# A graph layer's edge loop: the first set's sorting drawn in smaller portions over more parts, and dst compared with node numbers by tensor_tensor from PSUM

## Chip, cores and metric

The kernel runs on one core of one Trainium2 chip. The metric is the device time of one execution in microseconds, as the median of several executions; less is better. Beside it stands one profiled execution, from which every duration below is taken. The engines are named as the profile has them: PE (TensorE matmul), PEld (its weight load), DVE (VectorE), ACT (ScalarE), POOL (GpSimd) and SP (SyncE, here a queue that issues DMAs).

## The reference

x has 12500 nodes of 128 features. There are 412500 edges (200000 random pairs in both directions and a loop at each node), sorted by dst.

```python
theta = x[dst] - x[src]
w = sigmoid(relu(theta @ W1 + b1) @ W2 + b2)
w_theta = w * theta
agg = segment_sum(w_theta, dst, num_segments=n_nodes)
indeg = segment_sum(ones((dst.shape[0], 1)), dst, num_segments=n_nodes)
out = layernorm(x + agg + indeg * (x @ W4 + b4))
```

Since (x[dst] - x[src]) @ W1 is x[dst] @ W1 - x[src] @ W1, the product is needed once for each node and not once for each edge.

## The kernel before

**Table.** The nodes are taken in 14 chunks of up to 1024. `table_chunk` loads rows of x, turns them on PE (L607), multiplies by W1 (L612), and stores x @ W1 beside x in the DRAM table z, one row of 256 floats for a node (DVE copies the product, L615, ACT copies x, L616, SP stores, L617).

**Parts and blocks.** The edges are cut into 372 parts of up to 1024, handled as 8 tiles of 128 edges; two parts make a block, whose dst lie within 96 consecutive nodes. `gather(s)` issues eight indirect DMAs on POOL's queue (L328), each fetching 128 rows by the indices of the part's src: out of x for parts 0 to 7 (`NH = 8`), out of z from part 8 on. A gather of part s also waits until the compute of part s - 6 (`LAG`) has come to the corresponding place (`steps_of`); the main loop calls `gather(s + 4)` (`AHEAD`) in part s. For parts 0 to 7 each gather waits for a step of the table instead, so that they spread over it. The gathered rows lie in nine buffers.

In the loop over parts, a part's compute is: `one_hot` builds oh, a matrix that has a one where an edge belongs to one of three groups of 41 nodes' places; `spread_y` multiplies it with the block's own product y (L714), which gives each edge its dst's product in PSUM; `weights` subtracts the gathered product (DVE L757), applies relu and w2 (L758), sums (L761), and scales the gathered rows by the sigmoid (ACT L762, L764); `one_hot_w` compares 96 node places with each edge's dst (L724) and `add_up` sums the scaled rows by node on PE (L827). Parts 0 to 7 compute the product themselves from the gathered x (`both`, L735 to L742) in place of L757. Each block also has picks for y (`part_y`, L670 to L680), a compare of edges to often used rows that stay in SBUF (`hot_one_hot`, L779 and L784), and its own totals (`total`, of which L843 writes the columns `own`) and normalization.

**Sorting.** Parts 0 to 17 (`PLAIN`) take their edges as they are stored. The other 354 parts belong to three sets of 128, 128 and 98 parts, each of which is prepared at once by the generator `place`: each partition holds one part's 1116 edges; edges to the 1152 first nodes are taken out (64 of the largest keys by `max` and `match_replace`, L483 and L485), the others are moved together. Its steps are drawn with `next(steps)`, and each runs to the next `yield`. There are 79 draws for a set: 1 for columns, 3 for differences (which use the PSUM tile pw), 3 for keys, 16 for max and replace in turn, 1 for the hot edges (which stores hot_d), 6 for counts (pw again), 42 for shifting (seven rounds of six; L543, L545 and L547, whose scratch `bits` lies in PSUM), 1 that stores off_d, 1 that unpacks src, 4 for transposes into src_i and rel, and the last, which hands the set over. Part 18 is the first that uses the first set: its gathers, issued in the loop's part 14, need src_i, and the fetch of its block, in the same part, reads off_d and hot_d back.

The first set's draws stand behind table chunks 2 to 13 and at the head of the loop's first parts; the second and third set are drawn once a part, from parts 25 and 153 on.

**Order.** Instructions are emitted in the order of this program. SP's queue keeps that order exactly; on the other engines a planner may move an instruction ahead where its inputs allow. `after` puts what it holds behind given instructions of the same engine.

**The tile fix.** One PSUM tile of 512 columns holds constants and scratch: `iota_f` (96 columns, read by L724), `own` (128, written by ACT L843 and DVE L848), `nid` (9, read by L779) and the rest as `bits`, of which the shift uses up to 272 columns.

In parts from 18 on, `one_hot` compares `to_all` (the dst places of the part's edges, bf16 in SBUF, the same on all partitions) with `place_c` (one number per partition, SBUF) by one `tensor_scalar` of 123 x 1024 (L705).

The draws in the program:

```python
        while len(done) < len(chunks):
            chunk()
            gather_first()
            with after(done[-1]):
                for _ in range(6):
                    next(steps, None)
...
            if s % 2 == 0 or s < PLAIN - 3:
                for _ in range(3 if s < NH else 1):
                    next(steps, None)
```

Of the kernel before, what the change touches and what calls it, by code (L numbers as in the profile page):

```python
# [11 lines left out]
I32 = mybir.dt.int32  # L12
U16 = mybir.dt.uint16
AF = mybir.ActivationFunctionType
OP = mybir.AluOpType
# [3 lines left out]
P = 128  # L19
D = 128  # L20
# [3 lines left out]
WB = 96  # L24
SW = 41
# [8 lines left out]
NH = 8  # L34
FIRST = P // K
MORE = 2
PLAIN = FIRST + MORE
HS = 64
HT = 9
# [9 lines left out]
def gnn_resnorm(  # L49
# [37 lines left out]
    nc = tc.nc  # L87
# [10 lines left out]
    chunks = [(n0, P, TC) for n0 in range(0, N - P * TC + 1, P * TC)]  # L98
# [22 lines left out]
    def set_of(s):  # L121

        s0 = 0 if s < PLAIN else PLAIN + (s - PLAIN) // P * P
        return placed[s0], s - s0
# [76 lines left out]
    fix = cps.tile([P, 512], F32, name="fix")  # L201
    iota_f = fix[:, :WB].rearrange("p (o m) -> p o m", o=1)
    own = fix[:, WB:WB + D]
    nid = fix[:, WB + D:WB + D + HT]
    bits = fix[:, WB + D + HT:].bitcast(I32)
    w2_f = w2_r.rearrange("p (o m) -> p o m", o=1)

    YB = WB + 3
# [3 lines left out]
    def constants():  # L212

        nc.vector.tensor_copy(ident_b, ident)
        nc.vector.tensor_scalar_mul(wneg, wts[:, 0, :], -1.0)
        nc.scalar.activation(fix[:, :WB], iota_row[:, :WB], AF.Copy)

        def at_least(name, n, v=1.0):
            c = const.tile([P, 1], F32, name=name)
            nc.vector.tensor_scalar(c, iota_p, float(n), v, op0=OP.is_ge, op1=OP.mult)  # L220
            return c

        ge = [at_least(f"ge{i}", i * SW) for i in range(4)]
        m12 = const.tile([P, 1], F32, name="m12")
        nc.vector.tensor_sub(m12, ge[3], ge[1])
        m2 = const.tile([P, 1], F32, name="m2")
        nc.vector.tensor_sub(m2, ge[3], ge[2])


        for t in oh_buf:  # L230
            nc.vector.memset(t, 1.0)
        nc.vector.memset(to, 1.0)
        place_c = const.tile([P, 1], F32, name="place_c")
        nc.vector.tensor_add(place_c, ge[1], ge[2])
        nc.vector.tensor_scalar(place_c, place_c, -float(SW), None, op0=OP.mult)
        nc.vector.tensor_add(place_c, place_c, iota_p)

        yu_buf = [const.tile([P, 2, D], F32, name=f"yu{i}") for i in range(5)]
        bh = const.tile([P, D], BF16, name="bh")
        b1_s = const.tile([P, D], F32, name="b1_s")  # L240
        e_c = const.tile([P, 1], F32, name="e_c")
        nc.vector.memset(b1_s, 0.0)
        for i in range(3):
            nc.vector.tensor_copy(bh, b1_r)
            nc.vector.tensor_scalar(e_c, iota_p, float(WB + i), None, op0=OP.is_equal)
            nc.vector.scalar_tensor_tensor(b1_s, bh, e_c, b1_s, op0=OP.mult, op1=OP.add)
            nc.vector.tensor_sub(b1_r, b1_r, bh)
        for t in yu_buf:
            nc.vector.tensor_copy(t[WB:, 0, :], b1_s[WB:, :])

        ones_b = const.tile([3, P], BF16, name="ones_b")
        nc.vector.memset(ones_b, 1.0)
        b4_3 = const.tile([3, D], BF16, name="b4_3")
        b4_s = const.tile([3, D], F32, name="b4_s")
        nc.vector.memset(b4_s, 0.0)
        for i in range(3):
            nc.vector.tensor_copy(bh[:3], b4_r[:3])
            nc.vector.tensor_scalar(e_c[:3], iota_p[:3], float(i), None, op0=OP.is_equal)
            nc.vector.scalar_tensor_tensor(b4_s, bh[:3], e_c[:3], b4_s, op0=OP.mult, op1=OP.add)
            nc.vector.tensor_sub(b4_r[:3], b4_r[:3], bh[:3])  # L260
        nc.vector.tensor_copy(b4_3, b4_s)


        behind = const.tile([P, P], F32, name="behind")
        nc.vector.memset(behind, -4.0)
        for i in range(3):
            nc.vector.tensor_copy(behind[:WB, i * SW:(i + 1) * SW], lag[:WB, :SW])
        at = behind[WB:, 3 * SW:3 * SW + 3]
        nc.vector.tensor_scalar(at, lag[WB:, 3 * SW:3 * SW + 3], float(WB - 3 * SW), 4.25,
                                op0=OP.is_equal, op1=OP.mult)  # L270
        nc.vector.tensor_scalar(at, at, -4.0, None, op0=OP.add)

        place_w = const.tile([P, 1], F32, name="place_w")
        nc.vector.tensor_scalar(place_w, iota_p, -float(P), None, op0=OP.add)
        node_c = const.tile([P, 1], F32, name="node_c")
        nc.vector.tensor_scalar(node_c, iota_p, float(HT), None, op0=OP.mult)
        nc.vector.tensor_scalar(nid, iota_row[:, :HT], node_c, None, op0=OP.add)

        pair = const.tile([P, P // SUB], BF16, name="pair")
        nc.vector.tensor_add(pair, ident[:, 0::2], ident[:, 1::2])  # L280
        turn = []
        for h in range(SUB):
            turn.append(const.tile([P, 1], F32, name=f"turn{h}"))
            nc.vector.tensor_reduce(turn[h], ident[:, h::2], AX.X, OP.add)
        most = const.tile([P, 1], F32, name="most")
        nc.vector.memset(most, float(SW + HS))
        apart = const.tile([P, PM], F32, name="apart")
        nc.vector.tensor_scalar(apart, iota_row[:, :PM], 2048.0, None, op0=OP.mult)
        return (place_c, m12, m2, yu_buf, behind, ones_b, b4_3,
                (place_w, pair, turn, apart, most))  # L290
# [15 lines left out]
    def tiles(s):  # L306
        return K if s < NF else KT
# [269 lines left out]
    with tc.manual_schedule(engines={SP}), tc.tile_pool(name="work", bufs=2) as wp, tc.tile_pool(  # L577
# [43 lines left out]
        @contextmanager  # L621
        def after(instructions):

            with ExitStack() as stack:
                for i in instructions:
                    stack.enter_context(tc.issue_after(i.ins))
                yield
# [56 lines left out]
        def one_hot(s, half):  # L684


            n0, n1 = half * G, min(half * G + G, tiles(s))
            if half == 0:
                parts[s] = {"oh": oh_buf[s % 2]}
            oh = parts[s]["oh"]  # L690
            if s < PLAIN:
                (_, _, off), i = set_of(s)
                pd = ps_l.tile([P, G, P], F32, name="pd")
                pd = pd.rearrange("p k e -> p (k e)").bitcast(BF16)
                pd = pd.rearrange("p (k e) -> p k e", e=P)[:, :G, :]
                for k in range(n0, n1):
                    nc.tensor.transpose(pd[:, k - n0, :], off[:, k, i:i + 1].to_broadcast([P, P]),
                                        ident_b)
                nc.vector.tensor_scalar(oh[:3 * SW, n0:n1, :], pd[:3 * SW, :n1 - n0, :],
                                        place_c[:3 * SW], None, op0=OP.is_equal)  # L700
            elif half == 0:
                n = tiles(s)
                b, h = divmod(s, SUB)
                at = blocks[b]["to_all"].rearrange("p h (k e) -> p h k e", e=P)
                nc.vector.tensor_scalar(oh[:3 * SW, :n, :], at[:3 * SW, h, :n, :],  # L705
                                        place_c[:3 * SW], None, op0=OP.is_equal)

        def spread_y(s):

# [172 lines left out]
        xts, done = [], []  # L882

        def chunk():
            c = len(done)
            xts.extend(table_load(i) for i in range(len(xts), min(c + 3, len(chunks))))
            done.append(table_chunk(c, xts[c]))
# [4 lines left out]
        def gather_first():  # L892

            while gathered[0] < AHEAD and (gathered[0] + 1) * len(chunks) <= (len(done) + 1) * NH:
                gather(gathered[0])
                gathered[0] += 1
# [8 lines left out]
        with after(done[1]):  # L905
            place_first_dst(0, FIRST, ps_l, dst_f)
            place_c, m12, m2, yu_buf, behind, ones_b, b4_3, hot_c = constants()
            place_w = hot_c[0]
# [5 lines left out]
        while len(done) < len(chunks):  # L914
            chunk()
            gather_first()
            with after(done[-1]):
                for _ in range(6):
                    next(steps, None)
        with after(done[7]):  # L920
            bases(FIRST, NS, ps_l)
# [5 lines left out]
        with after(done[9]):  # L927
            window(0)
            for s in (0, 1):
                one_hot(s, 0)  # L930
                one_hot(s, 1)
                if s == 0:
                    spread_y(0)
        for s in range(NS + 2):
# [7 lines left out]
                    hot_t, z[:HOT, :].rearrange("(p t) d -> p t d", t=HT))  # L942
                nc.scalar.activation(hot_t[:, :, :D], hot_t[:, :, :D], AF.Copy, scale=-1.0)
            if s % 2 == 0 or s < PLAIN - 3:
                for _ in range(3 if s < NH else 1):
                    next(steps, None)
            b = s // SUB
            if s % SUB == 0:
# [5 lines left out]
            if s >= NH and s + 2 < NS:  # L954
                one_hot(s + 2, 0)
# [228 lines left out]
```

## Time and profile before

| | us |
|---|---|
| median of three runs | 3919.13 (3914.03 to 3920.94) |
| the profiled execution, device time | 3919.01 |
| its span, first to last instruction | 3917.2 (mean granted clock 0.806) |

| engine | busy us | share of the span | instructions |
|---|---|---|---|
| PE | 2667.6 | 68% | 15349 |
| PEld | 2252.2 | 57% | 15349 |
| DVE | 2829.5 | 72% | 5501 |
| ACT | 1594.4 | 41% | 5226 |
| POOL | 2866.5 | 73% | 2978 |

The page's chain of waits, followed back from the last instruction, has 34% DVE, 22% DMA, 19% PE, 16% ACT, 6% issue and 2% POOL. It is to be read with care: at each step it goes to what released a wait last, and where several engines work in step it changes between them.

By stretches (from the busy times of windows, us of each engine):

| window | length | PE | DVE | ACT | POOL |
|---|---|---|---|---|---|
| 60 to 80 | 20 | 0.77 | 18.38 | 2.54 | 3.73 |
| 100 to 120 | 20 | 15.48 | 13.16 | 6.86 | 11.33 |
| 200 to 260 | 60 | 49.30 | 39.29 | 32.99 | 4.23 |
| 262 to 300 | 38 | 29.64 | 36.47 | 22.54 | 28.50 |
| 1180 to 1600 | 420 | 293.05 | 291.18 | 171.01 | 318.82 |
| 1695 to 1830 | 135 | 104.11 | 118.61 | 66.43 | 103.50 |
| 2540 to 3880 | 1340 | 934.69 | 909.20 | 534.81 | 1018.12 |

How to read it: a group's row on the page gives line, engine, operation, what is written from what, partitions x elements, count, then busy time and mean ns of one, then the idle time of the engine just before it and what ended most of that. "Busy" counts an instruction's own length; POOL's gathers are the making of descriptors, and the rows themselves arrive later by DMA. A window's row gives the length, then busy time and count of PE, PEld, DVE, ACT and POOL, the granted clock, the DMA engines' share and GB/s.

### The profile page before, as it was taken

To read this page: it belongs to the slowest core of one execution; us is meant where nothing else is said; L and a number is where in the kernel's file an instruction comes from. 1 tells how busy PE (TensorE), PEld (TensorE's weight loads), DVE (VectorE), ACT (ScalarE), POOL (GpSimd) and SP (SyncE) were. 2 spreads that over 40 slices of the span, in tenths; PEclk is the share of its full clock that TensorE was granted. 3 is DMA by queue.
4 is the path that set the end of the run, shared out by engine and by line. 5 is a ranking of instruction groups with operands and counts; after the bars stand their busy time and mean duration, and the time that the engine had idled before them with its cause. 6 is when DMAs were issued, how large, how long until landed. Compare 5 with 4: busy or idle time off the path is not lost.

```text
span 3917.2 us, 52459 instructions
## 1 busy us (share of the span) xinstructions
PE 2667.6 (68%) x15349; PEld 2252.2 (57%) x15349; DVE 2829.5 (72%) x5501; ACT 1594.4 (41%) x5226; POOL 2866.5 (73%) x2978
## 2 busy tenths in 40 slices
PE   3487776776667766667766776676766766767665
PEld 2366555555556655556555655566655656656554
DVE  6778787777767666669887777666666666666665
ACT  2254443434444343334444434444343443344443
POOL 3637777777777777777777777777777777777775
PEclk7698787877778888878887777878888888888887
DMA  5425444444444444445444444444445444444443
GB/s 179 138 66 163 138 138 142 142 144 143 139 143 143 142 143 142 133 143 150 143 140 138 142 141 146 142 139 139 141 142 144 142 141 138 142 143 144 141 136 98
DMA packets 242089, 547.83 MB, mean 140 GB/s; under 512 B 60819, under 2 KB 120893, under 8 KB 240129
## 3 DMA queue, kind: packets, MB, share of 16 engines
q0 software_dynamic: 141488, 385.15, 33.8%
q1 hardware_dynamic: 98335, 152.85, 12.9%
q10 hardware_dynamic: 1970, 6.40, 0.4%
q8 instruction: 123, 2.02, 0.2%
q14 instruction: 173, 1.42, 0.1%
HBM read 521.31 MB, written 22.85 MB: 139 GB/s over the span
## 4 chain that ended last, share of the span: by engine, by line
DVE 34%; DMA 22%; PE 19%; ACT 16%; issue 6%; POOL 2%; DVEq 0%; SPq 0%; ACTq 0%; POOLq 0%
DMA zbuf<-z,src_i 22%; PE pd L792 11%; ACT wx L764 10%; DVE ph L757 8%; DVE ph L758 8%; DVE lg L761 7%; PE pa L827 3%; ACT wx L762 2%; DVE of L779 2%; POOL zbuf L328 2%; DVE pw L676 1%; DVE ow L724 1%; PE pw L659 1%; ACT a L838 1%; DVE fix L848 1%
## 5 line engine op out<-in xcount | busy, mean ns | idle before, releaser
L328 POOL DMA_INDIRECT zbuf<-z,src_i x2825 | 2728.2, 966 | 860.9 <-issue 416.0
L792 PE MATMUL pd<-hot_t,of 128*128 128x256 f32 x3186 | 995.1, 482 | 187.5 <-DVE of L779 156.9
L757 DVE TENSOR_TENSOR ph<-ph,zbuf 128x1024 f32<-128x1024 f32 x364 | 446.7, 1227 | 846.3 <-DMA zbuf<-z,src_i 846.0
L792 PEld LDWEIGHTS pd<-hot_t,of 128*128 128x128 f32 x3186 | 777.8, 250 | 367.4 <-ACT wx L764 116.1
L827 PE MATMUL pa<-wx,ow 128*96 128x130 f32 x5938 | 905.6, 312 | 117.5 <-ACT a L838 109.3
L764 ACT ACTIVATE wx<-zbuf,wx 128x128 f32<-128x128 f32 x2969 | 910.8, 388 | 7.0
L827 PEld LDWEIGHTS pa<-wx,ow 128*96 128x96 f32 x5938 | 823.4, 192 | 153.6 <-ACT a L838 140.8
L714 PE MATMUL ph<-y,oh 128*128 128x128 bf16 x2905 | 292.5, 247 | 435.2 <-DVE y L680 287.6
L714 PEld LDWEIGHTS <-oh 128*128 128x128 bf16 x2905 | 236.4, 111 | 474.1 <-issue 342.1
L761 DVE TENSOR_REDUCE lg<-ph 128x8 f32<-128x1024 f32 x372 | 450.4, 1211 | 0.1
L758 DVE SCALAR_TENSOR_TENSOR ph<-ph,w_r 128x1024 f32<-128x1024 f32 x364 | 445.3, 1223 | 0.0
L838 ACT ACTIVATE a<-pa 96x130 f32<-96x130 f32 x186 | 50.4, 271 | 870.1 <-PE pa L827 870.0
L724 DVE TENSOR_TENSOR ow<-fix,rel 128x768 f32<-128x768 f32 x372 | 350.2, 942 | 12.0 <-ACT fix L843 5.9
L762 ACT ACTIVATE wx<-lg,b_c 128x8 f32<-128x8 f32 x372 | 112.2, 302 | 363.9 <-DVE lg L761 363.7
L779 DVE TENSOR_TENSOR of<-hot_all,fix 128x1152 f32<-128x1152 f32 x177 | 236.5, 1336 | 0.0
L678 ACT ACTIVATE ym<-pw 128x256 bf16<-128x256 f32 x186 | 70.6, 380 | 401.2 <-DVE pw L676 401.0
L827 PE MATMUL pa<-a,sh 96*96 96x130 f32 x370 | 87.5, 321 | 162.5 <-DVE sh L823 162.5
L705 DVE TENSOR_SCALAR oh<-to_all,place_c 123x1024 bf16<-123x1024 bf16 x354 | 169.9, 480 | 0.0
L672 PE MATMUL pw<-yu,pick 99*128 99x128 f32 x744 | 158.0, 335 | 13.1 <-ACT yu L662 5.8
L655 PE MATMUL pw<-ident,xw 96*128 96x96 f32 x186 | 54.8, 294 | 163.5 <-issue 120.5
L659 PE MATMUL pw<-wts,xwT 128*96 128x256 f32 x372 | 139.9, 462 | 37.6 <-ACT xwT L657 37.6
L827 PEld LDWEIGHTS pa<-a,sh 96*96 96x96 f32 x370 | 50.9, 174 | 191.6 <-DVE sh L823 189.4
(215 smaller groups left out, 2602.9 us busy)
## 6 DMA issues: line engine op xcount, KB each, us to landing
to_all<-off_d SPq DMA_DIRECT2D x177, 512.0 KB
zbuf<-z,src_i POOLq DMA_INDIRECT x2825
hot_all<-hot_d SPq DMA_DIRECT2D x177, 128.0 KB
z<-zbuf SPq DMA_DIRECT2D x12, 1024.0 KB
xw<-in_x_dram SPq DMA_DIRECT2D x186, 48.0 KB
out_dram<-o SPq DMA_DIRECT2D x186, 48.0 KB
zbuf<-in_x_dram ACTq DMA_DIRECT2D x12, 512.0 KB
zbuf<-z,src POOLq DMA_INDIRECT x80
```

The lines of the kernel that those rows point to most:

```text
L328: ins = nc.gpsimd.indirect_dma_start(out=rows_of(s)[:, k, :], out_offset=None, in_=z if s >= NH else x, in_offset=IndirectOffsetOnAxis(ap= ...
L659: nc.tensor.matmul(pw[:WB], xwT[:, :WB], wts, start=True, stop=False)
L714: got = nc.tensor.matmul(d["ph"][:, k, :], d["oh"][:, k, :], blocks[b]["y3"][h], start=True, stop=True)
L724: nc.vector.tensor_tensor(ow, iota_f.to_broadcast([P, n, WB]), rel[:, :n, i:i + 1].to_broadcast([P, n, WB]), op=OP.is_equal)
L757: nc.vector.tensor_sub(ph, ph, zs[:, :n, :D])
L758: nc.vector.scalar_tensor_tensor(h[:, :n, :], ph, 0.0, w2_f.to_broadcast([P, n, D]), op0=OP.max, op1=OP.mult)
L761: summed = nc.vector.tensor_reduce(lg[:, :n], h[:, :n, :], AX.X, OP.add)
L762: nc.scalar.activation(wx[:, :n, D], lg[:, :n], AF.Sigmoid, bias=b2_c)
L764: scaled = nc.scalar.activation(wx[:, k, :D], xs[:, k, :], AF.Copy, scale=wx[:, k, D:D + 1])
L779: nc.vector.tensor_tensor(d["of"].rearrange("p t (h e) -> p t h e", e=HS), at[:, :, 0, :, :].to_broadcast([P, HT, SUB, HS]), nid.rearrange ...
L792: nc.tensor.matmul(d["px"], d["of"][:, t, :], hot_t[:, t, :], start=t == 0, stop=False)
L827: summed = nc.tensor.matmul(pa, one, w, start=h == 0 and i == 0, stop=h == 1 and i == len(terms) - 1)
```

## The change

Three things are changed. The first set's draws are 2 behind each table chunk and 4 behind the last, instead of 6; in the loop they are 4 in each of parts 0 to 13, instead of 3 in parts 0 to 7 and 1 in parts 8 to 14. (From part 14 on nothing differs, since the condition around it then draws one in even parts, and another line one in odd parts, as before.) A column `node` of the PSUM tile fix takes a copy of place_c, and `bits` begins one column later. The compare of L705 becomes a `tensor_tensor` of `to_all` with that column, broadcast over all elements.

```diff
     nid = fix[:, WB + D:WB + D + HT]
-    bits = fix[:, WB + D + HT:].bitcast(I32)
+    node = fix[:, WB + D + HT:WB + D + HT + 1]
+    bits = fix[:, WB + D + HT + 1:].bitcast(I32)
...
         nc.vector.tensor_add(place_c, place_c, iota_p)
+        nc.vector.tensor_copy(node, place_c)
...
-                nc.vector.tensor_scalar(oh[:3 * SW, :n, :], at[:3 * SW, h, :n, :],
-                                        place_c[:3 * SW], None, op0=OP.is_equal)
+                nc.vector.tensor_tensor(
+                    oh[:3 * SW, :n, :], at[:3 * SW, h, :n, :],
+                    node[:3 * SW].rearrange("p (k e) -> p k e", e=1).to_broadcast([3 * SW, n, P]),
+                    op=OP.is_equal)
...
             with after(done[-1]):
-                for _ in range(6):
+                for _ in range(2 if len(done) < len(chunks) else 4):
                     next(steps, None)
...
             if s % 2 == 0 or s < PLAIN - 3:
-                for _ in range(3 if s < NH else 1):
+                for _ in range(4 if s < PLAIN - 4 else 1):
                     next(steps, None)
```

## The prediction

> **What bounds the kernel now.** I read the page's groups first, then each POOL row of the gathers' line, then a stretch of the timeline in the middle of the run, then the start.
>
> ```profile
> L328 POOL DMA_INDIRECT zbuf<-z,src_i x2825 | 2728.2, 966 | 860.9 <-issue 416.0
> L757 DVE TENSOR_TENSOR ph<-ph,zbuf 128x1024 f32<-128x1024 f32 x364 | 446.7, 1227 | 846.3 <-DMA zbuf<-z,src_i 846.0
> L724 DVE TENSOR_TENSOR ow<-fix,rel 128x768 f32<-128x768 f32 x372 | 350.2, 942 | 12.0 <-ACT fix L843 5.9
> L779 DVE TENSOR_TENSOR of<-hot_all,fix 128x1152 f32<-128x1152 f32 x177 | 236.5, 1336 | 0.0
> L705 DVE TENSOR_SCALAR oh<-to_all,place_c 123x1024 bf16<-123x1024 bf16 x354 | 169.9, 480 | 0.0
> ```
>
> No engine is over 73% busy, but POOL's idle is not free time. The line's own view gives the spread of one gather:
>
> ```profile
> L328 POOL DMA_INDIRECT zbuf<-z,src_i x2825: 942/947/1936, 301.6 to 3889.4; - x189
> ```
>
> The timeline (start, length, engine, line) shows gathers back to back, 0.30 us between one's end and the next's start:
>
> ```profile
> 1999.98 0.49 DVE L705 TENSOR_SCALAR oh<-to_all,place_c 123x1024 bf16<-123x1024 bf16 x1
> 2000.10 1.20 POOL L328 DMA_INDIRECT zbuf<-z,src_i  x1 [0.30 <-issue]
> 2001.60 0.95 POOL L328 DMA_INDIRECT zbuf<-z,src_i  x1 [0.31 <-ACT wx L764]
> ...
> 2007.81 0.47 DVE L705 TENSOR_SCALAR oh<-to_all,place_c 123x1024 bf16<-123x1024 bf16 x1
> 2007.86 1.24 POOL L328 DMA_INDIRECT zbuf<-z,src_i  x1 [0.30 <-issue]
> 2009.40 0.95 POOL L328 DMA_INDIRECT zbuf<-z,src_i  x1 [0.30 <-ACT wx L764]
> ```
>
> From the first gather of part 18 (301.6 us) to the last there is no other gap: 2825 x (0.947 + 0.305) = 3537 us, and the rows' excess over 0.947 adds 55; seen 301.6 to 3890.4, 3589. The gap's named releasers are noise, since it is 0.30 whoever is named. So **span = T18 + 3537 + excess + tail**, where T18 is the start of part 18's gathers (301.6), the excess 55 and the tail 27. DVE waits for gathers (846 us at L757); part s is finished some 7 us after its last gather, 42 us before gather s+6 needs its pace. Compute is not on the path there.
>
> The start is another stage. POOL stalls there, and PE stands still while DVE sorts (columns: length, then PE, PEld, DVE, ACT, POOL busy):
>
> ```profile
> POOL zbuf L328 <- ACT wx L764: 57.3, 16, 50.8
> POOL zbuf L328 <- PE pw L607: 48.6, 4, 16.4
> ```
> ```profile
> 140.00:160.00 20.00, 0.03 (x1) 0.00 (x0) 18.29 (x51) 0.00 (x0) 15.14 (x16) 0.50 0.37 106
> 220.00:240.00 20.00, 16.63 (x135) 14.00 (x134) 12.78 (x23) 11.47 (x36) 0.00 (x0) 1.00 0.01 4
> ```
>
> **The compare (L705), 354 times.** The two L705 rows above each lie on a gather that is 0.25 to 0.29 us long beyond its neighbours. Laying every gather of the long stage against the DVE rows of the timeline: 414 overlap an L705 row and hold 47.3 of the 55.4 us excess; 98 overlap a pick (L670) but no L705 and hold 4.3 (43 ns each); the 1812 that touch no tensor_scalar row of this loop hold 1.1, though L724 and L779, tensor_tensor with one operand in PSUM, lie on hundreds of them. So the new form should not stretch gathers. Of the 414, 128 also overlap a pick; left at the picks' own 43 ns they keep 5.5, and those with L784 0.3. **Gain 47.3 - 5.8 = 41 us.** Ends: if half of the excess of gathers that overlap both (23 us) stays with the pick, 36; if all goes, 47.
>
> The Trainium skill ("SBUF — State Buffer", Who interferes with whom) says that a VectorE operation in a two-port mode and GpSimd exclude each other for a whole instruction, and that one with at most one SBUF input outside these modes does not contend. By that rule each of 354 compares could hold POOL for its 0.48 us, 170 us in all; the rows say 47[...]. I take the rows.
>
> A rule speaks against the change: "VectorE: DVE Perf Modes" (the perf-mode tier table) gives tensor_scalar on bf16 in SBUF four elements a cycle and any tensor_tensor with a PSUM operand one. The rows agree: L724 and L779 fit 1.026 ns an element plus 0.154 us, so 1024 elements take 1.20 us against 0.48. That is +0.73 us x 354 = +257 us of DVE work. Were DVE the bound, this would be the result. But from 2540 to 3880 DVE is busy 909 of 1340 us, 6.88 us a part of 10.14; with 0.73 it is 7.6 of POOL's 8 x 1.252 = 10.02, and the 846 us of waiting for gathers cover it. The tightest place is after part 151, where the compute is 33 us behind the gathers and 19 us of pace are left: there DVE is busy 118.6 of 135 us while parts take 9.1 us; 9.1 + 0.73 is still below 10.02, so the backlog shrinks, only more slowly. Cost 0; at worst the 19 us run out and some 15 us of gathers are lost. The compare now reads the PSUM tile that L843 writes; L724 does too and waits 12 us in all for ACT, so about as much, hidden. The one tensor_copy more in the constants is 0.2 us at 25 us, and the shift of the scratch columns by one costs nothing.
>
> **The first set's sorting.** It has 79 draws. Before: 6 after each of twelve table chunks (72), the rest in parts 0 to 2. After: 11 x 2 + 4 = 26 in the table, then 4 a part: 52 in parts 0 to 12, the last in part 13. No instruction is added; its two stores on SP's queue are issued later, hot_d behind the last table store (before: between stores), off_d in part 11, ahead of the block loads, which run two blocks ahead.
>
> *Table.* POOL's first 64 gathers follow the table's transposes. They wait 15.6, 16.2 and 16.4 us at 30, 65 and 87 us, where the transposes wait for the PSUM tile pw that six draws in a row hold, and end at 136.3. With two draws a chunk, chunk 3 waits only for the first of the three difference loops (39 instead of 45.5 us, 9 us of stall left); a max and its replace are 2.8 us, a chunk's copy 1.2, together near the 3.5 us in which a chunk passes when little lies between. 4 + 64 x 1.252 + 9 = **93 us**.
>
> *Parts 0 to 7.* Before, DVE ends the sorting at 171.5, the first logits start 17.4 later, and parts follow every 9.72 us (188.9 to 256.9) with DVE busy 39.3 of 60 us, 6.35 a part. After: 93 + four count loops of 2.7 (10.7) + 17.4 = 121. The shift rounds cost 7.3 us for six draws, so 4.9 us a part: 11.25 busy. I take 11.8, DVE 95% full as between 262 and 300 (36.5 of 38); ends 11.25 and 14.6 (nothing fits beside). Seven periods and the last sum (1.2): 205. Part 14's gathers, which wait for part 8's pace, followed the end of part 7's sum by 1.4 us (258.2 to 259.6): now at 206.5, and parts 14 to 17 end at 246.6.
>
> *Parts 8 to 11* hold the last fourteen rounds: 17 us on top of 20.1 (258.2 to 278.3), so 242. Then the unpack, four ACT passes and two sets of transposes, 4.5 us, and queues ahead of them some 5: src_i at 252. What is late next is therefore not POOL (246.6) but the index itself. **T18 = 252, gain 50 us.** Ends: 238 (11.25 a part, start 9 us earlier) and 285 (14.6 a part, table or start 16 us late), gains 64 and 17. Later, compute takes parts in 6.2 to 8 us while POOL needs 10, so no pace wait follows.
>
> **Sum.** 3917.2 - 41 - 50 = 3826 of span. The profiled execution took 3919.0, 1.8 more than its span, and is 0.1 below the median: 3828.
>
> **Rivals.**
> - *Only the compare pays* (8%): sorting inside the parts exposes as much as it frees; 14.6 us a part, with a table still held by pw. For it: DVE is full at 262 to 300 already. Against: PE idle from 140 to 160, 40 us of DVE idle from 160 to 260. 3919 - 41 = 3878.
> - *Only the start pays* (6%): picks take over the hold. Against: the 98 gathers with a pick alone hold 4.3 us. 3919 - 50 = 3869.
> - *Nothing measurable* (3%): the holds stay and T18 does too, 3919.
> - *Slower* (5%): the new compare makes DVE the bound in every part from 18 on. It decides from a price of 10.02 - 6.40 = 3.6 us, and cancels the gain at 3.9 (91 / 354 = 0.26 more). If a PSUM operand held still took four cycles, 4.4 us: 0.78 x 354 = 276, 4104. Against: L779 reads held PSUM columns at 1.16 ns an element in all.
>
> The forecast has 78%, 3805 to 3868 from the ends (36 to 47, 17 to 64); the range goes to 3872 to take in the second rival. This kernel's runs differ by about 0.2%, which I take as no change: faster 92%, same 3%, slower 5%.
>
> **What would show it.** The compare's row at 1.15 to 1.3 us x354; DVE's total some 260 us up; gathers of the long stage at a mean of 0.947 to 0.955 (excess 5 to 20); their first start at 238 to 285; the 64th gather's end near 93 and no stall of 50 us before part 14; parts 1 to 7 every 11 to 15 us. Wrong if POOL shows gaps beyond 0.31 after part 18, if the gathers' mean stays at 0.966, or if part 18 starts after 300.

## The result, and the profile after

| | before | after |
|---|---|---|
| median, us | 3920.03 (3914.03 to 3921.8) | 3871.51 (3869.83 to 3873.45) |
| ratio, 95% interval | | 0.9879 [0.9862, 0.9896] |
| span of the profiled execution, us | 3917.2 | 3871.6 |
| start of part 18's gathers (T18) | 301.6 | 280.8 |
| from there to the end of the last gather | 3588.8 | 3559.8 |
| tail | 26.9 | 31.1 |
| DVE busy | 2829.5 | 3083.7 |

The kernel is faster by 48.5 us where 91 were forecast: a little more than half. All lines of the changed kernel's code stand 2 to 4 higher from here on (gathers L330, compare L707, sort's transposes L573, window's transpose L657). Its groups:

```profile
L330 POOL DMA_INDIRECT zbuf<-z,src_i x2825 | 2686.8, 951 | 873.3 <-issue 443.9
...
L761 DVE TENSOR_TENSOR ph<-ph,zbuf 128x1024 f32<-128x1024 f32 x364 | 447.5, 1229 | 367.5 <-DMA zbuf<-z,src_i 360.9
...
L707 DVE TENSOR_TENSOR oh<-to_all,fix 123x1024 bf16<-123x1024 bf16 x354 | 425.5, 1202 | 0.0
...
L728 DVE TENSOR_TENSOR ow<-fix,rel 128x768 f32<-128x768 f32 x372 | 347.6, 935 | 5.7 <-ACT fix L847 5.7
...
L783 DVE TENSOR_TENSOR of<-hot_all,fix 128x1152 f32<-128x1152 f32 x177 | 237.4, 1341 | 0.0
```

The compare has gone from 480 to 1202 ns, and a gather's mean from 966 to 951. The rows that did not change (L728, L783, L761) have kept their length. DVE's 256 us more of compares came out of its idle time: in all 1087.7 us before (3917.2 - 2829.5) and 787.9 now. Its wait for gathers at L761 fell even more, from 846 to 367.5, as a part of the idle time now stands before other instructions. DVE still waits for gathers, so it is not the bound over the run as a whole.

The gathers' own view gives min, median and longest, then first and last start:

```profile
L330 POOL DMA_INDIRECT zbuf<-z,src_i x2825: 942/949/1588, 280.8 to 3839.6; - x189
```

T18 is 280.8, inside the forecast's ends (238 to 285) but 29 later than its value. The chain of waits doesn't show why; POOL's waits between 236 and 285 us (total, times, longest) do:

```profile
POOL zbuf L330 <- PE pw L657: 26.5, 1, 26.5
```

One single wait of 26.5 us, for a transpose of `window` and not for the index. The timeline around it (start, length, engine, line; in brackets the idle time before and its releaser):

```profile
256.70 0.17 DVE L549 COPY_PREDICATED et<-fix,ew 128x12 f32<-128x12 int32 x1
...
258.61 0.66 PE L573 MATMUL pw<-ident,es 128*128 128x128 f32 x4 [1.34 <-ACT es L567]
...
260.84 0.57 ACT L575 ACTIVATE src_i<-pw 128x512 int32<-128x512 f32 x1
...
265.28 0.60 ACT L575 ACTIVATE rel<-pw 128x512 bf16<-128x512 f32 x1 [0.40 <-PE pw L573]
...
266.34 0.36 PE L657 MATMUL pw<-ident,xw 96*128 96x96 f32 x1
...
266.98 0.95 POOL L330 DMA_INDIRECT zbuf<-z,src  x1 [26.45 <-PE pw L657]
```

Read it from the end. The gather at 266.98 is tile 5 of part 16. By `steps_of` it waits for window(7)'s transpose of xw, which is emitted in part 12. Ahead of that transpose stand part 12's four draws: 26 in the table and 48 in parts 0 to 11 make 74, so these four are 75 to 78, the sort's four transposes. They use the PSUM tile pw, and so does the window: it gets it only when ACT has taken the fourth one out (265.28 + 0.60). So POOL waited for the whole sort in the middle of part 16, 5.6 us past the moment when the first half of src_i, all that part 18's first gathers need, was ready (260.84 + 0.57 = 261.41), and then still had to issue eleven gathers before part 18: 266.98 + 11 x 1.252 = 280.75.

The windows (length, then PE, PEld, DVE, ACT, POOL busy, clock) tell how DVE fared in the loop's first parts and at the sort's end:

```profile
145.00:210.00 65.00, 53.95 (x425) 45.69 (x426) 52.62 (x115) 35.06 (x101) 13.88 (x15) 0.97 0.17 53
...
237.00:257.00 20.00, 11.11 (x62) 9.77 (x61) 19.76 (x47) 6.25 (x21) 2.83 (x3) 0.59 0.11 27
```

In parts 0 to 7 DVE is 81% full; in the 20 us before the sort's last shift it is full, and parts 12 and 13, whose sums end by 250.0, shared it with the sort.

The other loss is far away, in parts 158 and 160, where the long stage had no gap before. POOL's rows:

```profile
1703.39 0.94 POOL L330 DMA_INDIRECT zbuf<-z,src_i  x1 [9.81 <-PE pw L657]
...
1726.84 0.95 POOL L330 DMA_INDIRECT zbuf<-z,src_i  x1 [2.87 <-PE pw L657]
```

Again window's transpose, and again tile 5, but now because xw comes late. SP's queue there, before (first fence) and after, shows the issue rows between two loads of xw. L143 and L146 load the third set's edges, and the L146 rows are its last part's, one partition alone; L150 loads bb, one number for each partition:

```profile
1625.96 0.34 SPq L633 DMA_DIRECT2D xw<-in_x_dram  x1
...
1634.96 0.33 SPq L143 DMA_DIRECT2D es<-in_src_dram  x1
1635.34 4.90 SPq L146 DMA_DIRECT2D es<-in_src_dram  x1
...
1651.55 1.58 SPq L146 DMA_DIRECT2D ed<-in_dst_dram  x1
1653.18 11.25 SPq L150 DMA_DIRECT2D bb<-in_dst_dram  x1
1665.54 2.47 SPq L633 DMA_DIRECT2D xw<-in_x_dram  x1
```

```profile
1601.29 0.34 SPq L635 DMA_DIRECT2D xw<-in_x_dram  x1
...
1619.83 0.30 SPq L143 DMA_DIRECT2D es<-in_src_dram  x1
1620.17 4.97 SPq L146 DMA_DIRECT2D es<-in_src_dram  x1
...
1626.05 12.19 SPq L146 DMA_DIRECT2D ed<-in_dst_dram  x1
1638.28 11.48 SPq L150 DMA_DIRECT2D bb<-in_dst_dram  x1
1650.86 2.68 SPq L635 DMA_DIRECT2D xw<-in_x_dram  x1
```

The two loads of xw are 39.6 us apart before and 49.6 after. One row, ed's, is 10.6 us longer, but that is not where the 10 us come from: before, the queue stood still for 11.0 us ahead of ed's rows, and after it does not. From the start of es's first row to the end of bb's, 29.5 us pass before and 29.9 after. The difference lies ahead of es: from the start of xw's row to that of es's it is 9.0 us before and 18.5 after. SP's wait at that load, in the kernel after, says what for:

```profile
SPq L143 <- DVE es L140: 13.7, 1, 13.7
```

L140 is a memset that clears es ahead of its load. The program emits it at the same place in both kernels, but it does not stand at the same place among DVE's instructions (before in the first fence, after in the second):

```profile
1168.72 0.99 DVE L140 MEMSET es<- 98x1116 int32 x1 [0.18 <-issue]
```

```profile
1618.81 0.99 DVE L140 MEMSET es<- 98x1116 int32 x1 [0.18 <-issue]
```

In PE's waits the transpose that needs the second xw waits 30.3 us before and 43.6 after. Before, the compute fell at most 32.8 us behind the gathers here, with 18.9 us of pace left; now it falls 54 behind, and 3.5 us are missing. Of these 21 us some 10 are the later load of es; another 10 were there already, since the first of the two loads of xw starts 36.1 us ahead of the end of part 151's gathers before and 25.8 after.

### The profile page after: what moved, and what is told of

The parts are those of the page before. It is cut to its first block, busy times and chain, and to the rows that moved or that the text cites. A ratio compares the mean times of both kernels' runs of the same rounds, so it can differ in the third digit from the quotient of the medians.

```text
span 3871.6 us, 52570 instructions
## 1 busy us (share of the span) xinstructions
PE 2639.7 (68%) x15349; PEld 2227.8 (58%) x15349; DVE 3083.7 (80%) x5502; ACT 1616.1 (42%) x5224; POOL 2826.3 (73%) x2978
## 4 chain that ended last, share of the span: by engine, by line
DVE 32%; PE 25%; DMA 16%; ACT 11%; issue 11%; POOL 3%; SPq 1%; DVEq 0%; POOLq 0%; ACTq 0%
DMA zbuf<-z,src_i 14%; PE pd L796 14%; ACT wx L768 7%; PE pa L831 6%; DVE ph L761 6%; DVE lg L765 5%; DVE ph L762 5%; DVE oh L707 3%; POOL zbuf L330 3%; DVE of L783 3%; DVE ow L728 3%; ACT wx L766 1%; DVE pw L678 1%; PE pw L674 1%; PE ph L718 1%
## 5 line engine op out<-in xcount | busy, mean ns | idle before, releaser
L330 POOL DMA_INDIRECT zbuf<-z,src_i x2825 | 2686.8, 951 | 873.3 <-issue 443.9
L796 PE MATMUL pd<-hot_t,of 128*128 128x256 f32 x3186 | 1014.8, 489 | 375.6 <-DVE of L783 375.3
L831 PE MATMUL pa<-wx,ow 128*96 128x130 f32 x5938 | 868.5, 311 | 182.2 <-ACT a L842 175.8
L761 DVE TENSOR_TENSOR ph<-ph,zbuf 128x1024 f32<-128x1024 f32 x364 | 447.5, 1229 | 367.5 <-DMA zbuf<-z,src_i 360.9
L707 DVE TENSOR_TENSOR oh<-to_all,fix 123x1024 bf16<-123x1024 bf16 x354 | 425.5, 1202 | 0.0
L718 PE MATMUL ph<-y,oh 128*128 128x128 bf16 x2905 | 265.4, 233 | 208.7 <-DVE oh L707 102.3
L728 DVE TENSOR_TENSOR ow<-fix,rel 128x768 f32<-128x768 f32 x372 | 347.6, 935 | 5.7 <-ACT fix L847 5.7
L718 PEld LDWEIGHTS <-oh 128*128 128x128 bf16 x2905 | 211.6, 104 | 234.5 <-DVE oh L707 108.5
L806 DVE SCALAR_TENSOR_TENSOR hh<-pd,w_r 128x128 f32<-128x128 f32 x177 | 51.1, 289 | 319.7 <-PE pd L798 319.7
L783 DVE TENSOR_TENSOR of<-hot_all,fix 128x1152 f32<-128x1152 f32 x177 | 237.4, 1341 | 0.0
L657 PE MATMUL pw<-ident,xw 96*128 96x96 f32 x186 | 52.2, 281 | 263.7 <-issue 190.5
L657 PEld LDWEIGHTS pw<-ident,xw 96*128 96x128 f32 x186 | 27.5, 148 | 279.9 <-issue 250.9
L808 ACT ACTIVATE wxh<-lgh,b_c 128x1 f32<-128x1 f32 x177 | 51.7, 292 | 314.0 <-DVE hh L806 312.5
L659 ACT ACTIVATE xwT<-pw 128x96 f32<-128x96 f32 x186 | 45.8, 246 | 309.4 <-PE pw L657 309.1
```

What stands on the lines that cost most here:

```text
L330: ins = nc.gpsimd.indirect_dma_start(out=rows_of(s)[:, k, :], out_offset=None, in_=z if s >= NH else x, in_offset=IndirectOffsetOnAxis(ap= ...
L707: nc.vector.tensor_tensor(oh[:3 * SW, :n, :], at[:3 * SW, h, :n, :], node[:3 * SW].rearrange("p (k e) -> p k e", e=1).to_broadcast([3 * SW ...
L718: got = nc.tensor.matmul(d["ph"][:, k, :], d["oh"][:, k, :], blocks[b]["y3"][h], start=True, stop=True)
L728: nc.vector.tensor_tensor(ow, iota_f.to_broadcast([P, n, WB]), rel[:, :n, i:i + 1].to_broadcast([P, n, WB]), op=OP.is_equal)
L761: nc.vector.tensor_sub(ph, ph, zs[:, :n, :D])
L783: nc.vector.tensor_tensor(d["of"].rearrange("p t (h e) -> p t h e", e=HS), at[:, :, 0, :, :].to_broadcast([P, HT, SUB, HS]), nid.rearrange ...
```

## The experiments

The parts in the sum are: T18 -20.8, the gathers' excess -42 (55.4 to 13.4, of what is over 0.947 us in each row), the two stalls +12.7 (with the usual 0.3 before each), the tail +4.2; together -45.9, where the span's change is -45.6 (3917.2 to 3871.6). **My theory:** the changes act side by side; the start is held by window(7) behind the sort, the stalls and the tail come from the longer compare. **Rivals:** DVE, now fuller, sets the start; or the 256 us of DVE work are on the path. All edits are against the kernel after.

**Each part alone.** draws_only keeps the new draws with the old compare; compare_only the old draws with the new compare.

```diff
-                nc.vector.tensor_tensor(
-                    oh[:3 * SW, :n, :], at[:3 * SW, h, :n, :],
-                    node[:3 * SW].rearrange("p (k e) -> p k e", e=1).to_broadcast([3 * SW, n, P]),
-                    op=OP.is_equal)
+                nc.vector.tensor_scalar(oh[:3 * SW, :n, :], at[:3 * SW, h, :n, :],
+                                        place_c[:3 * SW], None, op0=OP.is_equal)
```

> The new draws with the old compare (tensor_scalar, 0.48 us). If the two parts of the change add up: part 18's gathers start at 281 as in the changed kernel (stall of 26 us inside part 16 included), the gathers after that have an excess of 50 to 60 us over 0.947 again, POOL does not stall near part 158, tail 27: span 281 + 3537 + 55 + 27 = 3900, of which some 3892 to 3902. If instead the longer compare is what delays the start, part 18 starts before 270 here.

```diff
-                for _ in range(2 if len(done) < len(chunks) else 4):
+                for _ in range(6):
...
-                for _ in range(4 if s < PLAIN - 4 else 1):
+                for _ in range(3 if s < NH else 1):
```

> The old draws with the new compare. If the parts add up: part 18 starts at 301 to 303, the excess is 10 to 16 us, a stall of 5 to 15 us near part 158, tail 31: span 302 + 3537 + 13 + 12 + 31 = 3895 (3883 without the stall). If picks take over the hold when the draws stand elsewhere, the excess is over 30.

draws_only took 3895.91 us, ratio 0.994 [0.9924, 0.9957]; compare_only 3894.75, 0.9938 [0.9921, 0.9954]. The gathers' rows, of draws_only and then of compare_only:

```profile
L330 POOL DMA_INDIRECT zbuf<-z,src_i x2825 | 2726.5, 965 | 861.0 <-issue 429.8
```

```profile
L330 POOL DMA_INDIRECT zbuf<-z,src_i x2825 | 2684.6, 950 | 871.3 <-issue 447.7
```

With the old compare the rows stay long (965; excess 53.2) and T18 is 278.7, with the same stall in part 16; with the new one they are short (950; excess 14.4), T18 is 301.6 as before, and the stalls near part 158 (9.7 and 1.6 us) and a tail of about 31 are there. draws_only has neither stall; there es's memset stands at 1144 us, SP waits for it no more than before, and ed's row is 1.56 us. So the gains of 24.4 and 25.6 us add up to about the whole 48.5, and the later loss belongs to the compare, whether by its length or by the changed order on DVE.

**Where the start waits.** draws_behind_window emits a part's draws behind `window(b + 1)`, so that window(7) no longer stands behind the sort's transposes.

```diff
-            if s % 2 == 0 or s < PLAIN - 3:
-                for _ in range(4 if s < PLAIN - 4 else 1):
-                    next(steps, None)
             b = s // SUB
             if s % SUB == 0:
                 fetch(b + 2)
                 if b + 1 < NK:
                     window(b + 1)
+            if s % 2 == 0 or s < PLAIN - 3:
+                for _ in range(4 if s < PLAIN - 4 else 1):
+                    next(steps, None)
```

> The changed kernel with each part's draws placed behind fetch and window instead of ahead of them. Theory (pw order): part 16's sixth gather waits for window(7)'s transpose, which stands behind the four sort transposes in the one PSUM tile pw and so behind the end of the sorting. With window(7) ahead of them the 26 us stall in part 16 goes, part 18 then waits for its own indices: start 258 to 268, span 3851 to 3861. Rival (DVE full): the start is bound by all the work DVE has until part 13, and the stall only shows where it ends; then part 18 starts at 276 to 284 whatever the order, span within 5 of 3871.

3854.36 us, 0.9835 [0.9819, 0.9852]; span 3852.8, T18 266.4. The last of POOL's waits above the usual 0.3 us, between 200 and 300 us:

```profile
POOL zbuf L330 <- ACT src_i L575: 15.1, 1, 15.1
```

The stall in part 16 is gone; POOL now finishes parts 16 and 17 and then waits for the index, as the prediction had it. The sort itself ends 7 us later than in the kernel after (263.4 against 256.7), and T18 is 14 us earlier all the same. Of the later stalls one of 2.9 us is left, at part 160. "DVE is full" would have held T18 at 276 or later; it falls.

lag7 leaves the order and gives the gathers one part more of lead, LAG = 7 in place of 6.

```diff
-LAG = 6
+LAG = 7
```

> The changed kernel with a gather waiting for the part seven before it, not six. Theory (pace wait): the wait on window(7) falls on part 17's sixth gather, eight gathers later, so part 18 starts some 10 us earlier, at 271; the stall at part 158 (9.8 and 2.9 us), where compute is 54 us behind, goes, since the pace allows ten more: span 3871 - 10 - 13 = 3848. Rival (indices or DVE set the start): only the 13 us go, 3858 to 3862. If the pace is no limit anywhere, 3871.

3848.93 us, 0.9816 [0.98, 0.9832]; T18 270.8. The last of POOL's waits above the usual 0.3 us, between 100 and 310 us:

```profile
POOL zbuf L330 <- PE pw L657: 28.1, 1, 28.1
```

The wait is the same one, for the same transpose, but stands eight gathers later, at tile 5 of part 17: three gathers are left behind it instead of eleven. Eight gathers are 8 x 1.252 = 10.0 us, and T18 fell by 10.0. Of the two stalls 1.3 and 1.7 us are left (now in parts 159 and 161), although es's load waits as long as ever (13.7 us) and the compute falls as far behind (52 us). So the pace is what lets these delays through.

**Which property of the compare matters.** node_in_sbuf keeps the tensor_tensor but takes the node numbers from SBUF; twice issues the changed kernel's compare two times.

```diff
-                    node[:3 * SW].rearrange("p (k e) -> p k e", e=1).to_broadcast([3 * SW, n, P]),
+                    place_c[:3 * SW].rearrange("p (k e) -> p k e", e=1).to_broadcast([3 * SW, n, P]),
```

> The changed kernel, its compare still a tensor_tensor but against place_c in SBUF instead of the PSUM column. If leaving tensor_scalar's fast form is what frees POOL: the row stays near 1.20 us, the gathers' excess stays at 10 to 20 us, span within 6 of 3871. If the operand must lie in PSUM (two SBUF inputs hold POOL as the old form did): excess over 40, up to 354 x 1.2 us where a compare meets a gather, span 3900 or more.

```diff
                     op=OP.is_equal)
+                nc.vector.tensor_tensor(
+                    oh[:3 * SW, :n, :], at[:3 * SW, h, :n, :],
+                    node[:3 * SW].rearrange("p (k e) -> p k e", e=1).to_broadcast([3 * SW, n, P]),
+                    op=OP.is_equal)
```

> The changed kernel with the compare issued twice, 354 x 1.2 = 425 us of DVE work more, same output. Theory (POOL sets the pace, DVE's work is under cover): quiet parts keep 10.02 us, since DVE's 7.6 us a part become 8.8; in the two sorting stretches of some 79 parts each DVE comes near or over 10 us, so POOL stalls there, and the stall at part 158 grows: 3875 to 3950. If the compare were on the path: 3871 + 425 = 4296. Each case is read from POOL's gaps, stretch by stretch.

These two, and lag8 and lag8_three below, ran on another chip, where the kernel before itself takes 4866 us. There the engines pause for microseconds at a time, put down to "issue" or "remote": POOL stands still for 3 to 9 us 58 times in node_in_sbuf and 73 times in twice, once in the kernel after, and the gaps over 0.7 us between part 18's gathers and the last come to 640 and 998 us, against 13. The ratios (0.9828 [0.9805, 0.985] and 0.9967 [0.9956, 0.9979]) say nothing of what was asked: a kernel with longer gathers came out faster. The times are left undecided. The length of a row can still be read, since twice, with the PSUM operand, is a control on the same chip. The rows of node_in_sbuf, then of twice:

```profile
L330 POOL DMA_INDIRECT zbuf<-z,src_i x2825 | 2952.5, 1045 | 1441.7 <-issue 650.5
...
L707 DVE TENSOR_TENSOR oh<-to_all,place_c 123x1024 bf16<-123x1024 bf16 x354 | 428.8, 1211 | 80.2 <-remote 73.6
```

```profile
L330 POOL DMA_INDIRECT zbuf<-z,src_i x2825 | 2687.8, 951 | 1759.6 <-issue 712.2
```

With both operands in SBUF a gather takes 1045 ns in the mean, with one in PSUM 951, although the control issues twice as many compares. Laid against the DVE rows, the 443 gathers of node_in_sbuf that overlap a compare hold 273 of its 277 us over 0.947; in twice 940 gathers overlap one and hold 1.6. The difference, 2952.5 - 2687.8 = 264.7 us over 354 compares, is 0.75 us for each, more than the tensor_scalar ever cost (47.3 / 354 = 0.13). So tensor_tensor alone is not what frees POOL; the operand in PSUM is. The Trainium skill ("SBUF — State Buffer", Who interferes with whom) has an operation with two SBUF inputs contend with those GpSimd instructions that read SBUF, and infers that making descriptors is spared. A gather takes its indices from src_i in SBUF, and the rows here show that it is not spared; whether the reading of the indices is what collides was not tried.

twice_b is twice once more, on a chip where the kernel before takes 3916.06.

> The changed kernel with the compare issued twice, 354 x 1.2 = 425 us of DVE work more. Theory (POOL sets the pace, DVE's work is under cover): quiet parts keep 10.02 us, since DVE's 7.6 us a part become 8.8; in the two sorting stretches of some 79 parts each DVE comes near or over 10 us, so POOL stalls there: 3875 to 3950. If the compare were on the path: 3871 + 425 = 4296.

3889.0 us, 0.9931 [0.9914, 0.9947]. Its groups:

```profile
L330 POOL DMA_INDIRECT zbuf<-z,src_i x2825 | 2680.5, 949 | 897.5 <-issue 439.3
...
L765 DVE TENSOR_TENSOR ph<-ph,zbuf 128x1024 f32<-128x1024 f32 x364 | 444.6, 1221 | 190.4 <-DMA zbuf<-z,src_i 184.1
```

425 us more of DVE work cost 17.5 us (3889.0 - 3871.5; 20 by the two ratios), and the gathers keep their length (949). The stall at part 158 grows from 9.8 to 12.9, at 160 from 2.9 to 4.2, and four short ones come at parts 180 to 186 (4.1 to 7.9). DVE, now at 3468.7 of 3889.4 us, still waits 190 us for gathers. The rival that has the compare on the path would give 4296; POOL sets the pace, and DVE breaks through only where a set's loads and sorting pile up.

**Two parts more of lead, and faster tables.** lag8 has LAG = 8; lag8_three in addition draws 3 behind each chunk.

```diff
-LAG = 6
+LAG = 8
...
-                for _ in range(2 if len(done) < len(chunks) else 4):
+                for _ in range(3 if len(done) < len(chunks) else 4):
```

> The changed kernel with a gather waiting for the part eight before it. Theory (pace wait, then indices): window(7) falls on part 18's sixth gather, at 267, no later than it would come anyway; part 18 starts when its indices are there, 261 to 265; no stall near part 158. Span 263 + 3537 + 13 + 31 = 3844, 3838 to 3850. If buffers or DVE hold POOL as well: 3849 as with seven, or above.

> As lag8, with three draws behind each table chunk instead of two (37 instead of 26 in the table, the last in part 10). Theory: part 18 waits for the end of the sorting, which is 5 to 15 us earlier, since DVE is idle 11 us between 40 and 60 and 11 between 100 and 145 in the changed kernel: part 18 starts at 248 to 260, span 3825 to 3840. If the table, which six draws held up, is held again by three, the start moves back: 3844 or more.

4860.62 us, 0.9986 [0.997, 1.0003], and 4867.8, 1.0003 [0.9988, 1.0018], on the slower chip: inconclusive, for the reason above. They were run again as lag8_b and lag8_three_b on the chip of twice_b, and with 4 draws behind every chunk as lag8_four:

```diff
-LAG = 6
+LAG = 8
...
-                for _ in range(2 if len(done) < len(chunks) else 4):
+                for _ in range(4):
```

> The changed kernel with a gather waiting for the part eight before it. Theory (pace wait, then indices): window(7) falls on part 18's sixth gather, at 267, no later than it would come anyway; part 18 starts when its indices are there, 261 to 265; no stall near part 158. Span 263 + 3537 + 13 + 31 = 3844, 3838 to 3850. If buffers or DVE hold POOL as well: 3849 as with seven, or above. Holds where the kernel before takes its 3920.

> As lag8, with three draws behind each table chunk instead of two (37 instead of 26 in the table, the last in part 10). Theory: part 18 waits for the end of the sorting, which is 5 to 15 us earlier, since DVE is idle 11 us between 40 and 60 and 11 between 100 and 145 in the changed kernel: part 18 starts at 248 to 260, span 3825 to 3840. If the table is held again by three draws, the start moves back: 3844 or more.

> As lag8, with four draws behind each table chunk (48 in the table, the rest done in part 7). If DVE's work before part 18 alone set the start, it would not move against three draws (within 5 us). If the table's hold on pw counts, each further draw a chunk costs the 64th gather 5 to 12 us and parts 0 to 7 begin later: part 18 starts 5 to 20 us after that of three draws.

| | us | ratio [95%] | T18 | first gather out of z | sort's last shift |
|---|---|---|---|---|---|
| after (2 draws, LAG 6) | 3871.51 | 0.9879 [0.9862, 0.9896] | 280.8 | 102.7 | 256.7 |
| lag8_three_b | 3847.45 | 0.9823 [0.9807, 0.984] | 274.3 | 130.7 | 253.7 |
| lag8_four | 3842.21 | 0.9809 [0.9793, 0.9826] | 267.0 | 133.2 | 218.8 |
| lag8_b (2 draws) | 3835.3 | 0.9795 [0.9779, 0.9812] | 259.2 | 101.0 | 254.2 |

lag8_b is the best seen, and a little better than the 3838 to 3850 expected: no stall is left inside parts 16 and 17 or at 158. POOL still waits for its pace at the heads of parts 14 to 16 (17.0 us at most), but is done with part 17 at 229.8, and its last wait is the one for the index:

```profile
POOL zbuf L330 <- ACT src_i L575: 29.4, 1, 29.4
```

Its ratio to the kernel before lies below the changed kernel's with intervals apart. With three draws the table is held again; waits of POOL in the first 140 us, lag8_three_b:

```profile
POOL zbuf L330 <- PE pw L609: 40.3, 9, 12.0
```

In the kernel after that row is 15.8 us. Against lag8_b the sort ends only 0.5 us earlier, so there is nothing to win by it; the first hope written for it failed and its alternative held. And the old trap is back one step further on:

```profile
POOL zbuf L330 <- PE pw L657: 23.1, 1, 23.1
```

With 37 draws in the table and 40 in parts 0 to 9, all four of the sort's transposes stand ahead of window(6), which is emitted in part 10 and which tile 5 of part 16 waits for with LAG = 8. That gather starts at 260.6, and with it and the ten behind it T18 comes at 274.3. For lag8_four I expected T18 later than with three; it was 7 us earlier. There the sort's shifts are done at 218.8, no window stands behind its transposes when it counts, and the late parts 0 to 7 set the start instead: POOL waits 32.6 us at the head of part 16 for part 8's step. Two draws balance the two better than three or four.

## Why the prediction was half right

**The gathers' excess: right.** Forecast 41 us out of 55, measured 42 (55.4 to 13.4), the compare at 1.202 us for 1.20. In the kernel after, 637 gathers overlap one of the new compares and hold 2.0 us of the excess. The argument from L728 and L783, tensor_tensor rows that lie on gathers and don't stretch them, carried; node_in_sbuf shows that it rested on their operand in PSUM.

**T18: the step that failed.** It is the sentence "What is late next is therefore not POOL (246.6) but the index itself", and the 252 behind it. T18 came at 280.8, so 20.8 us were gained and not 50. The 29 us have two terms. The sort's last shift was put at 242 and came at 256.7: 14.7. I had given parts 8 to 11 the sort's remaining 17 us beside their own 20.1; DVE was full (19.76 of 20 us) but also took parts 12 and 13 ahead of the sort. And from there to T18 I had 10 us and it took 24.1: 14.1 more. I had counted the gathers of parts 14 to 17 as free after part 8's pace, though each waits for its own step six parts back; the step of part 16's tile 5 is a transpose emitted behind the sort's. The order of the emitted draws, 74 before part 12, was to be had from the diff. draws_behind_window and lag7 show this term by taking it away in two different ways (-14 and -10 us).

**The steps ahead of it.** The 64th gather was to end at 93 and ended at 102.4. The first logits were to start at 121 and started at 145.4: I had left out what remained of max and replace (about 8 us), two count draws, the bases and the first window's chain. The parts then passed every 9.14 us and not every 11.8, and the two errors cancelled: part 7's sum ended at 210.6 for 205, and part 14's first gather was at 212.7 for 206.5. That was luck: a right intermediate sum from two wrong terms gave no warning. One of the signs given, "no stall of 50 us before part 14", did not come true and could not by the prediction's own numbers: the 48 gathers after 93 are issued by 153, and part 14 was put at 206.5. POOL waits 49.5 us there.

**The cover of DVE's work: priced at 0, cost 12.7.** The place was named within seven parts ("the tightest place is after part 151", "at worst the 19 us run out"), but the sum took nothing for it, and gaps on POOL after part 18 were one of its signs of being wrong. The backlog was taken as 33 us and only slowly changed by 0.73 us a part; it was 54. About half of what was added is the order of DVE's instructions: es's memset stood at 1168.72 us and now stands at 1618.81, so that es's load, and behind it on SP's queue the next xw, came some 10 us later. In the ten traces on chips of like speed the memset stands at 1169 and 1144 us in the two kernels with the old compare, and in all eight with the new one 1.2 to 2.7 us ahead of ed's memset, with a wait of 13.8 us (17.6 in twice_b) for es's load. ed's row is 1.6 us in the first two and 11.7 to 12.2 in the eight, but where it is short the queue has stood still for 11 us just ahead of it, so nothing is lost by its length. Why the order changed, and what the stall would be with the memset early, is open: it was not tried alone.

**The tail: forecast unchanged, +4.2.** Compute ends further behind the last gather. compare_only has the same tail (31.3), draws_only the old one (26.6), and one compare more makes it 33.1 (twice_b), so it goes with the compare.

**The forecast and its rivals.** "Only the start pays" would have given 3869, close to 3871.5, but for the wrong reason: the compare's gathers paid as forecast, the start paid less than half of its 50, and later waits took a part back. That the time lies 0.5 us inside the upper end of 3872 is luck too: the range had been stretched to there for that rival. (The ends themselves add up to 3808 and 3866, not 3805 and 3868.) "DVE the bound in every part" did not come, and twice_b shows how far away it is.

## What to carry to other kernels

Where a queue's instructions are paced by other work, take the late gate as a list: for every paced instruction look up which instruction it waits for and what is emitted ahead of that on its engine and in its buffers. Freeing a shared PSUM tile in one place (the table) moves the same users to another place, and the first thing behind them there pays. When work is hidden under a margin, the price to write down is not 0 but what the margin still holds at its narrowest place, and there the order on every queue counts: here one memset of 1 us that came to stand later on DVE kept SP's loads back by some 10 us.

## What was not expected of the hardware

- A tensor_tensor of bf16 with both operands in SBUF lengthens the gathers' rows on POOL by 0.75 us for each compare of 1.21 us; with one operand in PSUM nothing of this is seen.
- Small DMAs can be long on the issuing queue, and the length is not the load's own: ed's load into one partition took 1.58 us where the queue had stood still for 11 us after es's, and 12.19 us where it followed at once. bb took 11.25 to 11.48 us behind it, and 0.62 to 0.65 us in the first two sets, which have no load into one partition. Most rows of SP take 0.3 to 0.4 us.
- The kernel before took 3916 to 3920 us in all other comparisons and 4866 on one chip, where the granted clock of the two kernels profiled as node_in_sbuf and twice was 0.74, against 0.80 for the kernel after; what makes the pauses there was not found.
